# Cross-attention with RWKV: attention's projections emitted in halves between its other matrix pieces

## The chip, the cores and the metric

The kernel runs on one core of one Trainium2 chip. The metric is the device time of one launch in microseconds (us); lower is better. Three runs of the kernel before gave 1450.99, 1446.82 and 1450.00 us, so the median is 1450.0 us.

## What is computed

Sixteen sequences (B = 16) of 112 tokens of width 512 pass through two layers. The first is a gated cross-attention to 375 context rows per sequence with 16 heads of 32:

```python
a = layer_norm(audio_kv, gamma, beta)
Q = hidden @ Wq.T;  K = a @ Wk.T;  V = a @ Wv.T            # heads of 32
attn = softmax(where(mask, Q K^T * 32**-0.5, -inf))
x1 = hidden + tanh(gate) * ((attn V) @ Wo.T)
```

The second is an RWKV block on x1: a layer norm, a mix with the token before (a low-rank tanh network gives five mixtures), projections r, k, v, g and a decay w, then a recurrence over the tokens for each head, s = k v^T + w s, out = r (u k v^T + s), a group norm, an output projection, and a feed-forward part with its own layer norm and three 512x512 projections. Everything is float32.

## The kernel before

**Data and pools.** Activations lie transposed: 512 channels are four chunks (NC = 4) of 128 partitions, and the tokens are the free dimension. Two sequences make a group (GB = 2, N = 224 columns), eight groups in all. A float32 matmul of the program is two instructions in the profile; a transpose is one. PSUM has eight banks: two for the tag `mm` (`ps_mm`, every projection, every transpose of the context, the attention's output piece `po`, the transposed sums `pbc`, all norms), four for the tag `s` (`ps_s`, scores, transposed probabilities and the front's `pxm`), one for `acc` and one for `w`. A tile of `mm` holds its bank from its first matmul until the engine that reads it out has done so.

**Four streams.** `attention` is one generator over all 16 sequences. For each group follow `front` (layer norm and mixing), `middle` (the recurrence on VectorE and GpSimd, with its projections and the sums `acc` on TensorE) and `back` (group norm, output projection, feed-forward). Each generator yields a cost after a piece; the loop at the end of the kernel always resumes the stream whose place is least, and adds the cost times a rate to that place (ATT = 92.0, FRONT, MIDDLE, BACK). So the order in which the source emits pieces is a merge of the streams by these costs. The framework then fixes each engine's static order: earlier emitted work has priority, but an instruction whose inputs or buffer are not there yet in its plan lets later ones pass. Evacuations from PSUM are marked `high_priority`. On the chip each engine runs its fixed order, and a late input stops all that is behind it on that engine.

**A step of attention.** Step i works on sequence b = i // 4 and head block m = i % 4 (four heads, one chunk of channels). It emits:

1. `scores(b, m)`: four matmuls `ps` (L298) with 32 rows each, which run side by side in four row strips of the array; VectorE adds the mask and takes the minimum (L309).
2. `outputs` (L348) for the block two steps back: twelve matmuls `po` with 32 columns each, four side by side; ScalarE copies them out to `oR` (L353).
3. `exponentials` on ScalarE (L318), planned behind that copy.
4. `transposed` (L329) for the block one step back, three times (c = 0, 1, 2), four transposes `pt` each; ScalarE or VectorE copies them out as `prT` (L336, L338).
5. Units of dense work for the next sequence, a quarter of them in each step: four `turn` (L219, transposes `pa` of the context), four `key` (L234, `pk`, eight instructions of 375 columns), three `value` (L245, `pv`, eight of 512), and every other sequence two `query` units (`pq`, L180, sixteen of 224).

When a block with m = 3 has had its outputs, `divide` forms the reciprocal of the softmax sums (GpSimd, VectorE, and a GpSimd copy `spread`, L364), transposes that (`pbc`, L367) and multiplies it into the outputs (L375). After the second sequence of a group two `out_project` units (`pp`, L180) follow, and VectorE adds them to x (L278), which opens the group's `front`.

**Where the units stand before the change.** A step takes its share of units as a list `mine` (three or four, padded with empty ones). After `outputs` comes, in a step with a finished sequence, `mine[0]` and then the whole of `divide`. Then, whole: the first of the remaining units ahead of the transposes c = 0, the transposes c = 1 directly behind those of c = 0, the next unit ahead of c = 2, and what is left behind c = 2. Nothing is emitted between `scores` and `outputs`.

```python
for c in range(NSC):
    if c != 1:
        mine[c // 2][1]()
        yield mine[c // 2][0]
    prTs.append(transposed(bb, bm, c, bprs))
    yield 0.5
```

Of the kernel before, what the change touches and what calls it, by code (L numbers as in the profile page):

```python
# [1 line left out]

# [11 lines left out]
P = 128  # L14
# [4 lines left out]
GB = 2  # L19
# [30 lines left out]
def xattn_rwkv_kernel(ctx: ExitStack, tc: tile.TileContext, ins: dict, out: bass.AP):  # L50
# [99 lines left out]
    def slab(name, mm):  # L150
        w = slabs.tile([P, NC, 2 * P], F32, tag="slab", name=f"{name}_{mm}")
        load = (nc.sync if heads else nc.scalar).dma_start(w, ins[name][mm])
        if len(heads) >= 5:
            planned_after(load, heads[-3])
        return w
# [15 lines left out]
    def mm_tile(name):  # L171
        return ps_mm.tile([P, 512], F32, tag="mm", name=name)

    def project(name, mm, rhs, label):

        w = first.pop(0) if first else slab(name, mm)
        ps = mm_tile(label)
        for e in range(2):
            for k in range(NC):
                mm_ = nc.tensor.matmul(  # L180
                    ps[:, e * N : (e + 1) * N], w[:, k, e * P : (e + 1) * P], rhs[:, k, :],
                    start=(k == 0), stop=(k == NC - 1),
                )
                if e == k == 0:
                    heads.append(mm_)
        return ps[:, : 2 * N].rearrange("p (e n) -> p e n", e=2)


    projected = set()

# [20 lines left out]
    def context_units(b):  # L211

        raw = raws.pop(b)
        aT = ctxp.tile([P, NC, S], F32, tag="aT", name=f"aT_{b}")

        def turn(k):
            pt = mm_tile(f"pa_{b}_{k}")
            for c in range(NSC):
                nc.tensor.transpose(  # L219
                    pt[:, c * SC : (c + 1) * SC], raw[:, c, k * P : (k + 1) * P],  # L220
                    ident[:SC, :SC],
                )
            with tc.high_priority(AHEAD):
                nc.scalar.activation(
                    aT[:, k, :], pt[:, :S], AF.Identity, bias=vec(R_B0, k), scale=vec(R_G0, k)
                )

        kTs[b] = kT = []
        vs[b] = v = kvp.tile([SC, NSC, D], F32, tag="v", name=f"v_{b}")

        def key(m):
            pk = mm_tile(f"pk_{b}_{m}")
            for k in range(NC):
                nc.tensor.matmul(  # L234
                    pk[:, :S], wk[:, k, m * P : (m + 1) * P], aT[:, k, :],
                    start=(k == 0), stop=(k == NC - 1),
                )
            kT.append(kvp.tile([P, S], F32, tag="kT", name=f"kT_{b}_{m}", bufs=6))
            with tc.high_priority(AHEAD):
                nc.scalar.copy(kT[m], pk[:, :S])  # L240

        def value(c):
            pv = mm_tile(f"pv_{b}_{c}")
            for k in range(NC):
                nc.tensor.matmul(  # L245
                    pv[:SC, :], aT[:, k, c * SC : (c + 1) * SC], wv[:, k, :],
                    start=(k == 0), stop=(k == NC - 1),
                )
            with tc.high_priority(AHEAD):
                nc.scalar.copy(v[:, c, :], pv[:SC, :])  # L250

        return (
            [(0.5, lambda k=k: turn(k)) for k in range(NC)]
            + [(2.6, lambda m=m: key(m)) for m in range(NC)]
            + [(3.5, lambda c=c: value(c)) for c in range(NSC)]
        )

    def query_units(g):
        qTs[g] = qT = kvp.tile([P, NC, N], F32, tag="qT", name=f"qT_{g}")

        def query(mm):
            pq = project("wq", mm, xg[g], f"pq_{g}_{mm}")

            with tc.high_priority(AHEAD):
                nc.scalar.activation(  # L265
                    qT[:, 2 * mm : 2 * mm + 2, :], pq, AF.Copy, scale=-(HD ** -0.5)
                )

        return [(3.0, lambda mm=mm: query(mm)) for mm in range(2)]

    def project_units(g):
        oT = qTs[g]

        def out_project(mm):
            pp = project("wo", mm, oT, f"pp_{g}_{mm}")
            x = xg[g][:, 2 * mm : 2 * mm + 2, :]
            with tc.high_priority(AHEAD):
                nc.vector.scalar_tensor_tensor(x, pp, tgate, x, ALU.mult, ALU.add)  # L278
            if mm == 1:
                projected.add(g)  # L280

        return [(3.0, lambda mm=mm: out_project(mm)) for mm in range(2)]

    masks, dens, mns = {}, {}, {}

# [66 lines left out]
        with tc.high_priority(AHEAD):  # L352
            return nc.scalar.copy(oR[:, m, :], po[:, :T])  # L353

    def divide(b, oR):

        rden = sm.tile([T, H0], F32, tag="rden", name=f"rden_{b}")

        nan = sm.tile([T, H0], F32, tag="nan", name=f"nan_{b}", bufs=1)
        nc.gpsimd.tensor_scalar(nan, mns.pop(b), 1e9, 0.0, ALU.mult, ALU.mult)  # L360
        nc.vector.tensor_tensor(rden, dens.pop(b), nan, ALU.add)
        nc.vector.reciprocal(rden, rden)
        spread = sm.tile([T, H0, HD], F32, tag="spread", name=f"spread_{b}", bufs=1)
        nc.gpsimd.tensor_copy(spread, rden.unsqueeze(2).broadcast_to([T, H0, HD]))  # L364
        pb = mm_tile(f"pbc_{b}")
        for m in range(NC):
            nc.tensor.transpose(  # L367
                pb[:, m * T : (m + 1) * T],
                spread[:, 4 * m : 4 * m + 4, :].rearrange("p h d -> p (h d)"),
                ident[:T, :T],  # L370
            )
        t0 = (b % GB) * T

        with tc.high_priority(AHEAD):
            nc.vector.tensor_tensor(  # L375
                qTs[b // GB][:, :, t0 : t0 + T], pb[:, : NC * T].rearrange("p (m t) -> p m t", m=NC), oR,
                ALU.mult,
            )

    def attention():  # L380

        normalise(0)
        for cost, unit in query_units(0) + context_units(0):
            unit()
            yield cost
        load_ahead(1)
        normalise(1, heads[-1])
        units, before, ready, oR = [], None, None, None
        for i in range(NC * B + 2):
            b, m = divmod(i, NC)  # L390
            if i < NC * B:
                if m == 0:
                    g = b // GB
                    if b % GB == 0 and g + 1 < NG:
                        xg[g + 1] = load_x(g + 1)
                    if b + 1 < B:
                        units += context_units(b + 1)
                        if (b + 1) % GB == 0:
                            units += query_units(g + 1)
                prs, score = scores(b, m)  # L400
                if m == 2 and b + 2 < B:
                    load_ahead(b + 2, score)
                if m == 3 and b + 2 < B:
                    normalise(b + 2, score)
                yield 0.9
            copied = None
            if ready:
                bb, bm, prTs = ready
                if bm == 0:
                    oR = kvp.tile([P, NC, T], F32, tag="oR", name=f"oR_{bb}", bufs=1)  # L410
                copied = outputs(bb, bm, prTs, oR)
            if i < NC * B:
                exponentials(b, m, prs, copied)
            if ready:
                yield 0.8
            todo = -(-len(units) // (NC - m)) if i < NC * B else len(units)
            mine, units = units[:todo], units[todo:]
            mine = mine + [(0.0, lambda: None)] * (3 - len(mine))
            if ready and bm == NC - 1:
                mine[0][1]()  # L420
                yield mine[0][0]
                mine[0] = (0.0, lambda: None)
                divide(bb, oR)
                yield 0.6
                if bb % GB == GB - 1:
                    mine = mine[1:2] + project_units(bb // GB) + mine[2:]
            ready = None
            if before:
                bb, bm, bprs = before
                prTs = []  # L430
                for c in range(NSC):
                    if c != 1:
                        mine[c // 2][1]()
                        yield mine[c // 2][0]
                    prTs.append(transposed(bb, bm, c, bprs))
                    yield 0.5
                ready = bb, bm, prTs
                mine = mine[2:]
            for cost, unit in mine:
                unit()  # L440
                yield cost
            before = (b, m, prs) if i < NC * B else None
        for cost, unit in units:
            unit()
            yield cost
# [574 lines left out]
```

## Time and profile before

| | us |
|---|---|
| runs shown: median (lowest to highest) | 1450.0 (1446.82 to 1450.99) |
| the profiled execution, its own time | 1452.38 |
| its span, first to last instruction | 1450.5 |
| TensorE matmuls busy, of the span | 1342.6 (93%) |
| VectorE busy | 915.7 (63%) |
| ScalarE busy | 657.9 (45%) |
| GpSimd busy | 659.5 (45%) |
| mean granted TensorE clock | 0.968 |

How to read it: PE is TensorE's matmuls, PEld its weight loads, DVE VectorE, ACT ScalarE, POOL GpSimd. The profile covers one execution. A busy PE is a modelled figure: matmuls are pipelined, and the record of one is longer than its distance to the next, so stretches of work are measured here from start to start. The first 50 us load weights and prepare the first sequence; from about 270 to 1108 us the pattern repeats about every 168 us, once per group; attention's last matmul starts at 1237.53 us, and what follows belongs to the last groups' middle and back.

### The profile page before, as it was taken

How to read it: one execution, taken by the hardware profiler on the slowest of the kernel's cores; microseconds unless marked ns; L12 is line 12 of the kernel's file. 1: busy time of each engine (PE TensorE's matmuls, PEld its weight loads, DVE VectorE, ACT ScalarE, POOL GpSimd, SP SyncE). 2: the span in 40 equal slices, each digit the busy share in tenths (PEclk: the TensorE clock that was granted, in tenths of full speed). 3: DMA queues.
4: the chain of work that ended last, by engine and by line, in shares of the span. 5: the costliest groups of instructions: out<-in, count | busy, mean ns of one | idle time of the engine just before them, and what ended most of it. 6: DMA issues, size and time to landing. Idle time of an engine off the chain costs nothing.

```text
span 1450.5 us, 23365 instructions
## 1 busy us (share of the span) xinstructions
PE 1342.6 (93%) x8516; PEld 951.4 (66%) x8516; DVE 915.7 (63%) x1750; ACT 657.9 (45%) x1527; POOL 659.5 (45%) x639
## 2 busy tenths in 40 slices
PE   6999999999999999999999999999999898788777
PEld 4557575657676676757677576866767476567546
DVE  1344647884668747765757847686567638884852
ACT  1454442564436543455525644356535345423342
POOL 2000326742656336542555426563465516664750
PEclk8999999999999999999999999999999999989979
DMA  7212024513554045431554135451545124535541
GB/s 210 78 52 68 14 90 146 161 41 102 155 162 161 30 132 165 150 103 51 175 165 149 42 102 173 143 161 30 152 155 162 46 84 133 164 112 158 168 134 56
DMA packets 116587, 171.79 MB, mean 118 GB/s; under 512 B 9770, under 2 KB 89514, under 8 KB 116346
## 3 DMA queue, kind: packets, MB, share of 16 engines
q1 hardware_dynamic: 113578, 168.11, 37.9%
q10 hardware_dynamic: 2832, 2.10, 0.5%
q8 instruction: 67, 1.10, 0.3%
q14 instruction: 46, 0.38, 0.1%
q0 software_dynamic: 64, 0.10, 0.0%
HBM read 162.95 MB, written 7.34 MB: 117 GB/s over the span
## 4 chain that ended last, share of the span: by engine, by line
PE 68%; DVE 11%; DMA 7%; ACT 5%; POOL 4%; issue 3%; SPq 2%; DVEq 0%; ACTq 0%; POOLq 0%
PE pv L245 9%; PE pk L234 9%; PE pt L329 5%; PE ps L298 5%; DMA kv<-vd 4%; PE pfv L180 3%; PE pfk L180 3%; PE pfr L180 3%; PE po L180 3%; PE acc L770 3%; DVE st L754 3%; PE pq L180 3%; PE pr L180 2%; PE pg L180 2%; PE pv L180 2%
## 5 line engine op out<-in xcount | busy, mean ns | idle before, releaser
L758 POOL TENSOR_TENSOR st<-st,r 128x448 f32<-128x448 f32 x256 | 322.0, 1272 | 208.1 <-DVE st L754 200.7
L754 DVE TENSOR_TENSOR_SCAN st<-wp,kv 128x448 f32<-128x448 f32 x256 | 267.9, 1076 | 106.5 <-ACT qT L265 33.3
L731 POOL TENSOR_TENSOR kv<-kv,k 128x444 f32<-128x444 f32 x128 | 153.4, 1201 | 95.2 <-DMA kv<-vd 94.5
L234 PE MATMUL pk<-aT,wk 128*128 128x375 f32 x512 | 182.7, 501 | 12.0 <-ACT oR L353 11.1
L245 PE MATMUL pv<-wv,aT 128*125 128x512 f32 x384 | 175.6, 601 | 1.5 <-ACT v L250 1.0
L309 DVE CUSTOM_DVE_ANT_0 pr<-ps,mb 112x375 f32<-112x375 f32 x256 | 128.0, 542 | 58.2 <-PE ps L298 58.0
L318 ACT ACTIVATE pr<-pr,mn 112x375 f32<-112x375 f32 x256 | 153.1, 601 | 4.2 <-DVE mn L309 4.1
L234 PEld LDWEIGHTS pk<-aT,wk 128*128 128x128 f32 x512 | 97.4, 198 | 70.6 <-ACT oR L353 12.8
L329 PEld LDWEIGHTS pt<-ident,pr 112*125 112x125 f32 x768 | 103.2, 190 | 36.6 <-issue 16.2
L329 PE MATMUL pt<-ident,pr 112*125 112x112 f32 x768 | 114.2, 279 | 6.1 <-DVE xm L558 5.7
L245 PEld LDWEIGHTS pv<-wv,aT 128*125 128x125 f32 x384 | 68.8, 188 | 77.8 <-issue 73.7
L731 DVE TENSOR_TENSOR kv<-kv,k 128x444 f32<-128x444 f32 x128 | 108.8, 850 | 3.3 <-DMA kv<-vd 2.1
L770 PE MATMUL acc<-st,consts 128*32 128x224 f32 x1024 | 78.3, 374 | 11.0 <-POOL st L758 9.3
L298 PE MATMUL ps<-kT,qT 32*112 32x375 f32 x512 | 84.8, 528 | 1.8 <-DVE xm L558 0.9
L466 ACT ACT_TABLE_LOAD x64 | 82.1, 1283 | 1.1
L564 POOL TENSOR_TENSOR xm<-xm,xa 128x448 f32<-128x448 f32 x48 | 59.1, 1247 | 37.9 <-DVE xm L558 37.8
L338 DVE COPY prT<-pt 125x448 f32<-125x448 f32 x80 | 49.1, 614 | 42.5 <-PE pt L329 42.5
L336 ACT COPY prT<-pt 125x448 f32<-125x448 f32 x112 | 59.1, 528 | 28.0 <-PE pt L329 27.7
L290 POOL TENSOR_SCALAR mb<-mrow 112x375 f32<-112x375 uint8 x16 | 8.9, 556 | 132.6 <-DVE mn L309 132.0
L180 PE MATMUL pfk<-xk,wfk 128*128 128x224 f32 x256 | 55.9, 372 | 10.9 <-DVE xk L857 5.6
L558 DVE SCALAR_TENSOR_TENSOR xm<-pxm,vecs,sx 128x224 f32<-128x224 f32 x128 | 47.4, 442 | 29.1 <-PE pxm L581 29.1
L240 ACT COPY kT<-pk 128x375 f32<-128x375 f32 x64 | 30.0, 469 | 72.6 <-PE pk L234 71.8
(146 smaller groups left out, 2354.0 us busy)
## 6 DMA issues: line engine op xcount, KB each, us to landing
kv<-vd SPq DMA_DIRECT2D x512, 111.5 KB
wo<-in_wo SPq DMA_DIRECT2D x32, 512.0 KB
ctx<-in_ctx SPq DMA_DIRECT2D x15, 750.0 KB
wv<-in_wv SPq DMA_DIRECT2D x16, 512.0 KB
wk<-in_wk SPq DMA_DIRECT2D x16, 512.0 KB
wr<-in_wr SPq DMA_DIRECT2D x16, 512.0 KB
wg<-in_wg SPq DMA_DIRECT2D x16, 512.0 KB
wfk<-in_wfk SPq DMA_DIRECT2D x16, 512.0 KB
```

The lines of the kernel that those rows point to most:

```text
L180: mm_ = nc.tensor.matmul(ps[:, e * N : (e + 1) * N], w[:, k, e * P : (e + 1) * P], rhs[:, k, :], start=(k == 0), stop=(k == NC - 1),)
L234: nc.tensor.matmul(pk[:, :S], wk[:, k, m * P : (m + 1) * P], aT[:, k, :], start=(k == 0), stop=(k == NC - 1),)
L245: nc.tensor.matmul(pv[:SC, :], aT[:, k, c * SC : (c + 1) * SC], wv[:, k, :], start=(k == 0), stop=(k == NC - 1),)
L298: score = nc.tensor.matmul(ps[:T, :S], qT[r : r + HD, m, t0 : t0 + T], kT[r : r + HD, :], start=True, stop=True,)
L309: nc.vector.tensor_tensor_reduce(pr, pss[hh][:T, :S], mb, 1.0, 3.0e38, ALU.add, ALU.min, mn)
L318: exp = nc.scalar.activation(pr, pr, AF.Exp, bias=mns[b][:, h : h + 1], scale=-1.0, accum_out=dens[b][:, h : h + 1],)
L329: nc.tensor.transpose(pt[:SC, hh * T : (hh + 1) * T], prs[hh][:, c * SC : (c + 1) * SC], ident[:T, :T])
L466: nc.scalar.preload_act_table_set(table)
L731: product = engine.tensor_tensor(kv4[:, two(p), :, 1:T], kv4[:, two(p), :, 1:T], k_prev.unsqueeze(1).broadcast_to([P, 2, GB, T - 1]), ALU. ...
L754: scan = nc.vector.tensor_tensor_scan(flat(pair), w_ps[c], flat(kv[:, two(p), :]), 0.0, ALU.mult, ALU.add)
L758: nc.gpsimd.tensor_tensor(pair, pair, rs[c // 2][:, c % 2, :].unsqueeze(1).broadcast_to([P, 2, N]), ALU.mult,)
L770: part = nc.tensor.matmul(accs[c][32 * q : 32 * q + 32, :], consts[:, C_WIN + 32 * e : C_WIN + 32 * e + 32], st[:, q, :], start=(e == 0), ...
```

## The change

Key, value, query and output projections become two units each instead of one. A half of a key or value holds two of the four matmuls over the contraction, so its `mm` tile stays open between the halves; a half of a query or output projection holds one of its two blocks of 128 output columns, again in one tile. The copy out stays behind the second half. The halves' costs are half the old ones (1.3, 1.75, 1.5), so a sequence's sum is as before. The context's transposes (`turn`) stay whole.

A step now spreads its share of units evenly: some behind `scores`, some behind `outputs`, some behind each of the three groups of transposes, and some behind `divide`, mostly one half each. `divide` is cut in two: `sums_spread` (the GpSimd and VectorE part) is emitted directly behind `outputs`, and the rest behind the first group of transposes. The output projection's four halves are put behind the first unit that is then left.

```diff
+    def project_halves(cost, name, mm, rhs, label, then):
+        def half(e, state):
+            if e == 0:
+                state["w"] = first.pop(0) if first else slab(name, mm)
+                state["ps"] = mm_tile(label)
+            w, ps = state["w"], state["ps"]
+            for k in range(NC):
+                mm_ = nc.tensor.matmul(
+                    ps[:, e * N : (e + 1) * N], w[:, k, e * P : (e + 1) * P], rhs[:, k, :],
...
+            if e == 1:
+                then(ps[:, : 2 * N].rearrange("p (e n) -> p e n", e=2))
...
-        def key(m):
-            pk = mm_tile(f"pk_{b}_{m}")
-            for k in range(NC):
+        def key(m, half, state):
+            if half == 0:
+                state["ps"] = mm_tile(f"pk_{b}_{m}")
+            pk = state["ps"]
+            for k in (2 * half, 2 * half + 1):
...
+            todo = -(-len(units) // (NC - m)) if i < NC * B else len(units)
+            dense = deque(units[:todo])
+            units = units[todo:]
+            slots = 1 + (2 if ready else 0) + (NSC if before else 0)
+            slots += bool(ready and ready[1] == NC - 1)
+            def fill():
+                nonlocal slots
+                share = -(-len(dense) // slots)
+                slots -= 1
+                for _ in range(share):
+                    cost, unit = dense.popleft()
+                    unit()
+                    yield cost
+            yield from fill()
             copied = None
             if ready:
                 bb, bm, prTs = ready
...
             if ready:
+                if bm == NC - 1:
+                    sums_spread(bb)
                 yield 0.8
+                yield from fill()
+            last = ready and bm == NC - 1
+            ready = None
+            for c in range(NSC if before else 0):
+                if c == 0:
+                    prTs = []
+                if c == 1 and last:
+                    divide(bb, oR)
+                    yield 0.6
+                    if bb % GB == GB - 1:
+                        rest = list(dense)
+                        dense = deque(rest[:1] + project_units(bb // GB) + rest[1:])
+                    yield from fill()
+                prTs.append(transposed(*before[:2], c, before[2]))
+                yield 0.5
+                yield from fill()
```

More of the change, by code (lines that the diff above doesn't have):

```diff
@@ L1 @@
+from collections import deque
 from contextlib import ExitStack
@@ L186, in project @@
         return ps[:, : 2 * N].rearrange("p (e n) -> p e n", e=2)
+    def project_halves(cost, name, mm, rhs, label, then):
[7 more added lines that the diff above has]
+                    ps[:, e * N : (e + 1) * N], w[:, k, e * P : (e + 1) * P], rhs[:, k, :],
+                    start=(k == 0), stop=(k == NC - 1),
+                )
+                if e == k == 0:
+                    heads.append(mm_)
+            if e == 1:
+                then(ps[:, : 2 * N].rearrange("p (e n) -> p e n", e=2))
+        state = {}
+        return [(cost, lambda e=e: half(e, state)) for e in range(2)]
     projected = set()
@@ L237, in key, with value @@
                 )
[L238 to L244, printed above, removed]
+            if half == 1:
+                kT.append(kvp.tile([P, S], F32, tag="kT", name=f"kT_{b}_{m}", bufs=6))
+                with tc.high_priority(AHEAD):
+                    nc.scalar.copy(kT[m], pk[:, :S])
+        def value(c, half, state):
+            if half == 0:
+                state["ps"] = mm_tile(f"pv_{b}_{c}")
+            pv = state["ps"]
+            for k in (2 * half, 2 * half + 1):
                 nc.tensor.matmul(
@@ L248, in value, with halves @@
                 )
-            with tc.high_priority(AHEAD):
-                nc.scalar.copy(v[:, c, :], pv[:SC, :])
+            if half == 1:
+                with tc.high_priority(AHEAD):
+                    nc.scalar.copy(v[:, c, :], pv[:SC, :])
+        def halves(cost, part, i):
+            state = {}
+            return [(cost, lambda h=h: part(i, h, state)) for h in range(2)]
         return (
             [(0.5, lambda k=k: turn(k)) for k in range(NC)]
-            + [(2.6, lambda m=m: key(m)) for m in range(NC)]
-            + [(3.5, lambda c=c: value(c)) for c in range(NSC)]
+            + [half for m in range(NC) for half in halves(1.3, key, m)]
+            + [half for c in range(NSC) for half in halves(1.75, value, c)]
         )
@@ L259, in query_units, with copied @@
         qTs[g] = qT = kvp.tile([P, NC, N], F32, tag="qT", name=f"qT_{g}")
-        def query(mm):
-            pq = project("wq", mm, xg[g], f"pq_{g}_{mm}")
+        def copied(mm, pq):
             with tc.high_priority(AHEAD):
@@ L267, in query, with added @@
                 )
-        return [(3.0, lambda mm=mm: query(mm)) for mm in range(2)]
+        return [
+            half for mm in range(2)
+            for half in project_halves(
+                1.5, "wq", mm, xg[g], f"pq_{g}_{mm}", lambda pq, mm=mm: copied(mm, pq)
+            )
+        ]
     def project_units(g):
         oT = qTs[g]
-        def out_project(mm):
-            pp = project("wo", mm, oT, f"pp_{g}_{mm}")
+        def added(mm, pp):
             x = xg[g][:, 2 * mm : 2 * mm + 2, :]
@@ L280, in out_project @@
                 projected.add(g)
-        return [(3.0, lambda mm=mm: out_project(mm)) for mm in range(2)]
+        return [
+            half for mm in range(2)
+            for half in project_halves(
+                1.5, "wo", mm, oT, f"pp_{g}_{mm}", lambda pp, mm=mm: added(mm, pp)
+            )
+        ]
     masks, dens, mns = {}, {}, {}
@@ L353, in outputs, with sums_spread @@
             return nc.scalar.copy(oR[:, m, :], po[:, :T])
-    def divide(b, oR):
+    spreads = {}
+    def sums_spread(b):
         rden = sm.tile([T, H0], F32, tag="rden", name=f"rden_{b}")
@@ L362, in divide @@
         nc.vector.reciprocal(rden, rden)
-        spread = sm.tile([T, H0, HD], F32, tag="spread", name=f"spread_{b}", bufs=1)
+        spreads[b] = spread = sm.tile([T, H0, HD], F32, tag="spread", name=f"spread_{b}", bufs=1)
         nc.gpsimd.tensor_copy(spread, rden.unsqueeze(2).broadcast_to([T, H0, HD]))
+    def divide(b, oR):
+        spread = spreads.pop(b)
         pb = mm_tile(f"pbc_{b}")
@@ L414, in attention @@
             if ready:
+                if bm == NC - 1:
+                    sums_spread(bb)
                 yield 0.8
[L416 to L422, printed above, removed]
+                yield from fill()
[14 more added lines that the diff above has]
+                yield from fill()
+            if before:
+                ready = (*before[:2], prTs)
+            elif last:
                 divide(bb, oR)
@@ L425, in attention @@
                 if bb % GB == GB - 1:
[L426 to L439, printed above, removed]
+                    dense.extend(project_units(bb // GB))
+            while dense:
+                cost, unit = dense.popleft()
                 unit()
```

## The prediction

> **What bounds the kernel now.** I read the page's shares first, then the stages in the table of windows, then TensorE's waits, then single stretches of the timeline.
>
> ```profile
> PE 1342.6 (93%) x8516; PEld 951.4 (66%) x8516; DVE 915.7 (63%) x1750; ACT 657.9 (45%) x1527; POOL 659.5 (45%) x639
> PE   6999999999999999999999999999999898788777
> ```
>
> TensorE is busy in nine tenths or more of every slice from about 36 to 1120 us, and no other engine comes near it. The tail is different: 7s and 8s, a chain of the last groups' norms and recurrence.
>
> ```profile
> 436.00:604.00 168.00, 162.89 (x1078) 116.21 (x1077) 114.81 (x221) 84.69 (x199) 83.02 (x78) 1.00 0.40 125
> 1240.00:1450.00 210.00, 164.33 (x907) 129.97 (x906) 132.34 (x186) 73.24 (x134) 112.86 (x94) 0.90 0.43 132
> ```
>
> The columns are the window and its length, busy time of PE, PEld, DVE, ACT and POOL, granted clock, DMA share. One group's period of 168 us has 162.9 us of TensorE: about 5 us idle, 3%. Filling an idle array can win only those 5 us a period, and attention has no part in the last 210 us, which it only starts earlier or later. Which idle time is it?
>
> ```profile
> PE pk L234 <- ACT oR L353: 11.1, 5, 2.5
> PE ln_mean L488 <- POOL xa L483: 8.1, 7, 2.3
> PE pt L329 <- DVE xm L558: 5.7, 13, 0.9
> PE pfk L180 <- ACT v L250: 2.4, 4, 0.8
> PE pv L245 <- ACT v L250: 1.0, 1, 1.0
> PE pk L234 <- ACT kT L240: 0.8, 1, 0.8
> ```
>
> Each line gives who waited for whom, us in total, times, the longest. The first is no missing data: a key projection does not read oR. It waits for an `mm` bank, which the copy of `po` has to free. So do the last three; these four make 15.3 us. The second is the front's norm waiting for GpSimd, the third four `s` banks held by the front. Not one line shows a transpose waiting for exponentials or an output piece waiting for copies of the probabilities for longer than 0.9 us: **the pieces that the change puts work behind are already covered**, by whole units and by the other three streams.
>
> The long wait in the timeline, first TensorE, then ScalarE:
>
> ```profile
> 701.79 0.90 PE L298 MATMUL ps<-kT,qT 32*112 32x375 f32 x8
> 702.62 0.78 PE L348 MATMUL po<-prT,v 125*32 125x112 f32 x24
> 703.34 3.29 PE L180 MATMUL pk<-xm,wk 128*128 128x224 f32 x16
> 708.78 3.67 PE L234 MATMUL pk<-aT,wk 128*128 128x375 f32 x7 [2.15 <-ACT oR L353]
> ```
> ```profile
> 706.64 1.04 ACT L853 ACTIVATE xk<-xc,vecs,mix_by 128x222 f32<-128x222 f32 x2 [3.77 <-DVE xc L506]
> 707.58 1.02 ACT L853 ACTIVATE xr<-xc,vecs,mix_by 128x222 f32<-128x222 f32 x2
> 708.51 0.23 ACT L353 COPY oR<-po 128x112 f32<-128x112 f32 x1
> ```
>
> `po` was done near 703.4, but its copy stood on ScalarE behind `xk` and `xr`, which waited 3.77 us for VectorE. A whole projection of the middle (3.3 us) ran in the other bank meanwhile, and then TensorE had none. It recurs at 372, 540, 709, 879 and 1044 us.
>
> **The change part by part.** It adds and removes no instruction: 8516 matmul records, the same copies, the same weight loads. The yielded costs have the same sums, so the streams' shares stay. What changes is order.
>
> 1. *Work between `ps` and `po`.* In the timeline of the whole run I count `po` directly behind `ps` 41 times (of 64 output pieces). A change between full-array matmuls and pieces that use strips costs time because the next weights are not loaded under the running matmul:
>
> ```profile
> 607.87 3.21 PE L180 MATMUL pp<-qT,wo 128*128 128x224 f32 x16
> 611.00 0.59 PE L770 MATMUL acc<-st,consts 128*32 128x224 f32 x8
> ```
> ```profile
> 191.49 3.03 PE pv L180 x16
> 194.51 3.03 PE pk L180 x16
> ```
>
> Sixteen instructions of 224 columns take 3.13 us to a strip piece's start (611.00 - 607.87) and 3.02 to another dense one's (194.51 - 191.49, chain of work): 0.11 us for the change, call it 0.10. `ps` to `po` pays one (rows to columns); `ps`, half, `po` pays two. So 41 x 0.10 = **+4.1 us**, all on TensorE's path; at most 64 x 0.10 = 6.4 if every step is split, and 0 if the planned order leaves no half there. The Trainium skill, in "TensorEngine Tiling (Array Packing)", section Key Properties, says that changing the tiling mode drains TensorE, which speaks against this edit and agrees in kind; it gives no price there. The page "TensorE: Matmul & The Clock Gate", Part 2, puts a drain at about 128 cycles, an estimate of 0.05 us, and the term would be about 2 us by it; the measured 0.10 goes into my sum.
>
> 2. *Halves behind transposes.* Four `pt` take 0.43 us before a dense piece (690.46 to 690.89) and eight take 0.86 between dense pieces (743.70 to 744.56 in the timeline): 0.11 each either way. No price: 0.
>
> 3. *An `mm` bank stays open between two halves.* This is the new wait. Before, a unit took a bank, filled it in 2.7 to 3.5 us, and the other bank was copied out meanwhile. Now a half holds one of two banks while `po`, `pbc` or another stream's projection goes through the other. There are 18 split units per group (8 keys, 6 values, 2 queries, 2 outputs), some 135 windows in the run once the first sequence is set up. `po` falls between two halves when a unit's first half stands behind `scores`, in about half of 62 steps: 30. Other streams take 30 `mm` tiles per group (front 4, middle 14, back 12, from the source) among attention's about 88 yields, 0.34 a yield, 0.7 in a window of two yields; so in about half of the 30, 15 times, a third tile asks for a bank while both are held. What waits behind it on TensorE is everything: it is one queue. If the static order runs the second half first, the price is 0. If not, it is at least the copy that frees the bank: 0.25 us for oR, 0.47 for kT, 0.53 to 0.59 for the others (the tiles' rows), and at most what the trace shows when ScalarE is late, 11.1/5 = 2.2 us. Ends: 0 and 15 x 2.2 = 33 us. I take kT's 0.47, because an order planned around buffers leaves the plain copy more often than a blocked ScalarE: 15 x 0.47 = **+7 us**.
>
> 4. *The existing bank waits.* The finer order may move the five coincidences apart, or make them worse: with a half as cover (1.3 us) instead of a whole projection (3.3), a copy that is 5 us late costs up to 2 us more each, 5 x 2.0 = +10. If they go, -11.1 us, and also clock: the granted clock in the 4 us behind the pauses at 372, 709 and 1044 was 0.57, 0.61 and 0.57, behind the other two 1.00. Three times some 1.7 us, -5 us. I take 0, since what causes them is VectorE's and ScalarE's order, which isn't touched. The Trainium skill ("TensorE: Matmul & The Clock Gate", Part 1) says that the clock falls after an idle window of about 3.4 us; here pauses of 2.15 to 2.45 us were followed by it. By the page pauses of this length cost no clock and the gain would be 11 us, by the trace 16.
>
> 5. *`sums_spread` earlier.* The same GpSimd copy (0.61 us) and VectorE pair (0.15 and 0.25 at 1222) move ahead of about two halves and one transposed group. They are queued ahead of some recurrence work, in which GpSimd is idle half the time (82 to 83 us busy of 168), so nothing is late. TensorE's `pbc` waits 0.3 us in all. Gain at most 0.3, loss at most 16 x 1.0 = 16 us if each delayed the recurrence and TensorE had no cover; I take 0.
>
> 6. *Weight loads.* wq and wo loads are issued on SP's queue at the first half, 30 loads moved by a few pieces among 512 recurrence loads. TensorE waits for a weight once, at the start (4.0 us). Covered; a 512 KB load at the 120 GB/s of the windows lasts 4.3 us, the price of one that came late. 0, with one or two of these in the range.
>
> Copies after key, value and query, and VectorE's additions after the output projection, stay behind the second half; what waits for them stays.
>
> Sum: 4.1 + 7 = +11 us, in the stretch to 1237 us, and the tail starts that much later. The profiled execution's own time is 1452.4 (span 1450.5), 2.4 above the median, so 1463 for such an execution and **1461** beside the median of 1450.
>
> **Rivals.** (a) *Better cover, faster.* Small dense pieces between all strips mean that the next bank request is never far behind a copy; the five pauses and their half-speed clock go, -16, against +4 for the changes of mode: -12, **1438**. For it: the pauses are coincidences of order, and order is what changes. Against: the other idle lines (the norm behind GpSimd, the front's four banks) do not touch attention's units, and the ceiling is 5 us a period. (b) *One bank instead of two.* Part 3 at its upper end, when ScalarE is late as at 708 us: 33 + 4 = +37, **1487**. It decides from more than about 5 of 15 cases being late. (c) *The order hardly changes*: the framework's plan already lets ready work pass, so halves come together again and the strips stay side by side: **1450**. Against: priorities follow emission, and the timeline shows pieces largely in emitted order.
>
> **How the numbers follow.** A measurement of this kernel can tell about 0.3% (4.35 us) from no change. Forecast of about +11, with all slower outcomes below the rival's: 0.42; (b) 0.12; (a) 0.35; (c) 0.11. Faster 0.35, same 0.11, slower 0.54. The signs are nearly balanced, because the pauses are coincidences. Within slower the likeliest range is 1455 to 1475. The range for 8 in 10 must take in (a) with one period's other 5 us gained, 1433, and (b), 1487.
>
> **What would show it.** Right: `ps` followed by a half and then `po` in most steps, and more changes between dense and strip pieces; more or longer TensorE waits on the copies oR, kT, v, qT or on other streams' evacuations; about the same `ln_mean` and `pxm` waits; periods of 169 to 170 us instead of 168. Wrong: the line "pk <- oR" gone with nothing in its place and periods below 167 (rival a), or `ps` and `po` still side by side (c). A change of the tail alone (after attention's last matmul) by more than 5 us would come from a cause that I haven't priced.

## The result, and the profile after

Four runs of the changed kernel have a median of 1521.7 us (1520.1 to 1526.6), four of the kernel before beside them 1448.4 us. The ratio is 1.051, with a 95% interval of 1.048 to 1.054: **slower by 5%**, 73 us. The sign of the forecast was right; the time lies well above its range (1433 to 1487). The profiled execution took 1522.3 us, with a span of 1520.5, so the two profiles are 70.0 us apart.

The first view is the page of the changed kernel: busy time by engine, TensorE's busy share in 40 slices, and the clock granted to it.

```profile
PE 1381.6 (91%) x8516; PEld 968.9 (64%) x8516; DVE 926.2 (61%) x1750; ACT 662.2 (44%) x1528; POOL 673.9 (44%) x639
PE   7999998999999899988999899998999889789787
PEclk8899999999999899998999999999999999989788
```

The number of matmuls is the same, but 39 us more of busy time stand in it, and more slices show an 8. Neither tells where the time went, so the next views are tables of windows: one group's period in the kernel before, then the same period and the last 210 us in the changed kernel (the columns are those of the prediction's table).

```profile
457.12:624.61 167.49, 161.30 (x1060) 115.14 (x1060) 113.19 (x216) 82.97 (x193) 83.01 (x79) 1.00 0.41 126
```
```profile
482.76:663.05 180.29, 168.03 (x1060) 118.54 (x1060) 114.07 (x217) 83.85 (x193) 84.73 (x79) 0.96 0.38 116
1310.00:1520.00 210.00, 169.46 (x893) 131.85 (x892) 136.75 (x187) 74.87 (x137) 114.38 (x94) 0.86 0.42 130
```

A period is the stretch from one group's front norm (`ln_mean`) to the next one's; its start is called a mark here. The same 1060 matmuls take 180.3 us, where the kernel before needs 167.5, and the granted clock is 0.96 instead of 1.00. The tail looks as before. Measured by these marks, the span's 70 us split into +25.6 up to the third mark, +46.4 in the four periods that follow (671.3 to 717.7) and -2 behind them. The loss is a toll on every group that overlaps attention.

I split the four periods by TensorE's records from start to start. Of the +46.4 us, **+30.0 are pauses** of over 0.15 us (19 pauses with 19.3 us before, 41 with 49.3 after), and **+16.0 are clock**: TensorE ran at half clock, outside pauses, for 13.6 us before and 45.6 after, and half of such a time is lost. All that is left, counted at full clock, stayed (645.2 us before, 645.7 after). So TensorE has no more work; it stands more often, and runs slowly behind that.

Who is waited for? The list of TensorE's waits in the changed kernel gives who waited for whom, us in total, times, the longest.

```profile
PE ln_mean L553 <- POOL xa L548: 11.7, 7, 1.9
PE pxm L646 <- DVE mn L349: 10.2, 5, 2.0
PE gm L690 <- DVE rden L403: 9.5, 5, 2.2
PE pfr L181 <- DVE own L762: 9.1, 5, 1.8
PE pt L369 <- DVE xm L623: 7.8, 8, 2.0
PE po L388 <- ACT k L721: 6.5, 5, 1.3
PE ps L338 <- ACT prT L376: 4.6, 6, 0.9
```

The old first line, `pk` behind `oR`, is gone. The wait for GpSimd's `xa` is still there (8.1 us before; in the four periods 6.3 before and 6.9 after). The other lines are new or have grown, and most come five times, once a group. By what ends them, the pauses per period are, in us before and after: an `mm` bank 2.6 and 3.9, an `s` bank 0.7 and 4.4, data 1.7 and 3.9. Only the first kind was priced.

**Two of the new pauses in the timeline** of the changed kernel. TensorE first; the brackets hold the pause ahead of an instruction and what ended it.

```profile
681.79 0.69 PE L369 MATMUL pt<-ident,pr 112*125 112x112 f32 x4
684.72 1.69 PE L690 MATMUL gm<-o,consts 128*128 128x448 f32 x2 [2.24 <-DVE rden L403]
...
699.38 0.88 PE L338 MATMUL ps<-kT,qT 32*112 32x375 f32 x2 [0.64 <-DVE mn L349]
699.85 1.11 PE L646 MATMUL pxm<-th,maa 32*128 32x224 f32 x8
702.99 1.86 PE L646 MATMUL pxm<-th,maa 32*128 32x224 f32 x8 [2.03 <-DVE mn L349]
```

And VectorE in the same stretch:

```profile
682.09 1.46 DVE L226 TENSOR_SCALAR ctx<-ctx,mv,rs 125x512 f32<-125x512 f32 x3 [1.09 <-POOL rs L224]
683.46 0.81 DVE L599 SCALAR_TENSOR_TENSOR mx<-sx,vecs,xa 128x224 f32<-128x224 f32 x2
684.19 0.38 DVE L843 TENSOR_TENSOR o<-acc,own 128x224 f32<-128x224 f32 x1
...
701.85 0.62 DVE L699 TENSOR_TENSOR o<-o,gsq 128x448 f32<-128x448 f32 x1 [1.59 <-ACT gsq L536]
702.39 0.54 DVE L349 CUSTOM_DVE_ANT_0 pr<-ps,mb 112x375 f32<-112x375 f32 x1
```

The group norm's matmul `gm` reads `o`. (The wait is put down to `rden`, which merely comes next on VectorE; `gm` starts 0.15 us after `o` is done.) `o` is an addition of 0.38 us whose sums `acc` TensorE had finished at 681.8. But on VectorE it stands behind the context's normalisation (`ctx`, L226), which waits for a GpSimd reciprocal root, and behind `mx`. In the kernel before the order is another. First TensorE, then VectorE:

```profile
640.44 0.96 PE L770 MATMUL acc<-st,consts 128*32 128x224 f32 x16
...
642.14 1.02 PE L625 MATMUL gm<-o,consts 128*128 128x448 f32 x2
```
```profile
641.47 0.39 DVE L778 TENSOR_TENSOR o<-acc,own 128x224 f32<-128x224 f32 x1 [0.98 <-PE acc L770]
...
648.89 1.46 DVE L204 TENSOR_SCALAR ctx<-ctx,mv,rs 125x512 f32<-125x512 f32 x3 [1.31 <-POOL rs L202]
```

`acc` is done at 641.4, `o` follows at once, `gm` starts without a pause, and the normalisation comes only at 648.9.

The second pause is one of `s` banks. `pxm` needs a bank which the last score minimum of four (L349) must free. Three minima are done by 700.3; the fourth stands behind `o<-o,gsq`, which waits 1.59 us for ScalarE. TensorE stands for 2.03 us, for an instruction of 0.54.

Now the clock behind these pauses, by the table of windows of the changed kernel (the number behind the five busy times is the granted clock):

```profile
685.00:689.00 4.00, 4.00 (x14) 2.69 (x17) 0.62 (x1) 1.88 (x3) 0.61 (x1) 0.59 0.02 4
703.00:707.00 4.00, 4.00 (x36) 2.73 (x37) 3.50 (x9) 2.49 (x4) 3.10 (x3) 0.50 0.00 0
```

TensorE is busy in every moment of both windows, at about half speed. In the four periods that is nearly all of its additional busy time (16.0 of 17.5 us).

Last, the pause that halving itself makes, in the timeline of the changed kernel:

```profile
779.71 1.78 PE L198 MATMUL pq<-x,wq 128*128 128x224 f32 x8
...
782.36 1.02 PE L760 MATMUL pruk<-own,consts 128*128 128x448 f32 x2
783.21 1.68 PE L198 MATMUL pq<-x,wq 128*128 128x224 f32 x8
786.71 3.29 PE L181 MATMUL pfr<-xr,wfr 128*128 128x224 f32 x16 [1.82 <-DVE own L762]
```

The first half of `pq` holds one `mm` bank from 779.7, and `pruk` takes the other. ScalarE has copied `pq` out by 785.5, yet `pfr` starts only when VectorE has read `pruk` out (`own`, done at 786.65). So `pfr` seems to be planned for that bank, and stands even while the other is free.

### The profile page after: what moved, and what is told of

The parts are those of the page before. It is cut to its first block, busy times and chain, and to the rows that moved or that the text cites. A ratio compares the mean times of both kernels' runs of the same rounds, so it can differ in the third digit from the quotient of the medians.

```text
span 1520.5 us, 23383 instructions
## 1 busy us (share of the span) xinstructions
PE 1381.6 (91%) x8516; PEld 968.9 (64%) x8516; DVE 926.2 (61%) x1750; ACT 662.2 (44%) x1528; POOL 673.9 (44%) x639
## 4 chain that ended last, share of the span: by engine, by line
PE 58%; DVE 17%; DMA 8%; ACT 5%; issue 5%; POOL 4%; SPq 2%; DVEq 0%; ACTq 0%; POOLq 0%
PE pk L258 10%; PE pv L272 7%; DMA kv<-vd 5%; DVE st L819 4%; PE pt L369 4%; PE pfr L181 3%; PE po L181 3%; PE pr L181 3%; PE pfv L181 2%; PE ps L338 2%; PE po L388 2%; PE acc L835 2%; PE pv L181 2%; PE pa L241 2%; PE pfk L181 2%
## 5 line engine op out<-in xcount | busy, mean ns | idle before, releaser
L258 PE MATMUL pk<-aT,wk 128*128 128x375 f32 x512 | 198.7, 510 | 0.1
L272 PE MATMUL pv<-wv,aT 128*125 128x512 f32 x384 | 188.0, 611 | 1.2 <-ACT oR L393 1.2
L796 POOL TENSOR_TENSOR kv<-kv,k 128x444 f32<-128x444 f32 x128 | 157.7, 1233 | 27.6 <-ACT prT L376 26.0
L349 DVE CUSTOM_DVE_ANT_0 pr<-ps,mb 112x375 f32<-112x375 f32 x256 | 127.0, 542 | 61.4 <-PE ps L338 61.4
L369 PEld LDWEIGHTS pt<-ident,pr 112*125 112x125 f32 x768 | 108.6, 191 | 47.2 <-issue 24.9
L258 PEld LDWEIGHTS pk<-aT,wk 128*128 128x128 f32 x512 | 92.5, 197 | 58.0 <-issue 22.3
L369 PE MATMUL pt<-ident,pr 112*125 112x112 f32 x768 | 118.3, 277 | 7.8 <-DVE xm L623 7.8
L835 PE MATMUL acc<-st,consts 128*32 128x224 f32 x1024 | 83.9, 379 | 8.2 <-DVE o L843 4.5
L338 PE MATMUL ps<-kT,qT 32*112 32x375 f32 x512 | 77.5, 524 | 10.7 <-ACT prT L376 4.6
L198 PE MATMUL pq<-x,wq 128*128 128x224 f32 x256 | 61.0, 385 | 8.8 <-DVE own L762 4.6
L181 PE MATMUL pfr<-xr,wfr 128*128 128x224 f32 x256 | 56.0, 375 | 13.3 <-DVE own L762 9.1
```

Source lines behind the costliest of these rows:

```text
L181: mm_ = nc.tensor.matmul(ps[:, e * N : (e + 1) * N], w[:, k, e * P : (e + 1) * P], rhs[:, k, :], start=(k == 0), stop=(k == NC - 1),)
L258: nc.tensor.matmul(pk[:, :S], wk[:, k, m * P : (m + 1) * P], aT[:, k, :], start=(k == 0), stop=(k == NC - 1),)
L272: nc.tensor.matmul(pv[:SC, :], aT[:, k, c * SC : (c + 1) * SC], wv[:, k, :], start=(k == 0), stop=(k == NC - 1),)
L338: score = nc.tensor.matmul(ps[:T, :S], qT[r : r + HD, m, t0 : t0 + T], kT[r : r + HD, :], start=True, stop=True,)
L349: nc.vector.tensor_tensor_reduce(pr, pss[hh][:T, :S], mb, 1.0, 3.0e38, ALU.add, ALU.min, mn)
L369: nc.tensor.transpose(pt[:SC, hh * T : (hh + 1) * T], prs[hh][:, c * SC : (c + 1) * SC], ident[:T, :T])
```

## The experiments

The change does four things at once, and each gives a theory. **Halving**: open `mm` banks between halves cost the time. **Places**: work now stands behind `scores`, behind `outputs` and between every two groups of transposes, so the `s` banks of a step are asked for at other times. **Division**: the sums are spread early and divided late. **Shares**: counted in halves, a first step takes five of 18 units, the four context transposes and a half, where it took three of eleven; so the steps' amounts of work differ. A fifth theory is that the rates of the merge (ATT against the other streams) merely fit the old source. Against all these stands a sixth: every edit of the order moves VectorE's and ScalarE's fixed orders, and no one part holds the loss.

Beside each ratio to the kernel before (95% interval) stand the pauses per period by kind (`mm` bank / `s` bank / data, in us; before 2.6 / 0.7 / 1.7, after 3.9 / 4.4 / 3.9) and the length of the period (167.8 and 179.4).

**1. Halves in the old places.** Both halves of a unit back to back where the whole stood, with a yield behind each (`run` emits the pieces of one unit so); the old division, the old shares.

```diff
-                        mine[c // 2][1]()
-                        yield mine[c // 2][0]
+                        yield from run(mine[c // 2])
```

> The changed kernel's halves, but both halves of a unit stand one behind the other at the places that whole units had before, with a yield between them; sums and division stand as before. Theory H (an open bank between halves makes the pauses): 1490 us or more, since another stream can still step between the halves. Theory P (the new places make them): 1445 to 1462. Theory S (any change of the merged order costs, whatever it is): 1480 or more.

Measured: 1464.9 us, 1.010 (1.007 to 1.013); pauses 5.7 / 0.3 / 2.1, period 170.4. The list of TensorE's waits of this kernel:

```profile
PE pk L258 <- ACT oR L393: 13.5, 5, 2.9
PE pfr L181 <- DVE own L743: 12.0, 5, 2.4
```

The old wait is still there, and `pfr` behind `own`, which the kernel before lacks, is added. So halving in the old places costs 1%, through `mm` banks (2.6 to 5.7).

**2. Whole units in the new places.** The changed kernel, with the two halves of a unit handed out as one.

```diff
-        return [(cost, lambda e=e: half(e, state)) for e in range(2)]
+        return [(2 * cost, lambda: [half(e, state) for e in range(2)])]
```

> Whole units again, but handed out by the changed kernel's rule: behind scores, behind outputs, behind single groups of transposes; sums early, division late. Theory H: no tile is open between pieces, so 1465 us or less. Theory P: 1490 or more. Theory S: 1480 or more.

Measured: 1521.8 us, 1.049 (1.046 to 1.052); pauses 5.4 / 0.4 / 5.4, period 180.8. As slow as the change, with no unit halved. Halving alone as the cause fell with these two. Pauses and clock make only 7.6 of the 13.0 us by which this period is longer than before. Some 4 more lie in the score matmuls, which more often start one behind the other than side by side (0.18 us from one to the next on average, 0.10 before), without a pause that counts.

**3 and 4. The rate of attention**, 96 instead of 92, in the kernel before and in the changed one; later also 88 in the changed one.

```diff
-ATT = 92.0
+ATT = 96.0
```

> The kernel before with one constant changed: attention's merge rate 1/96 instead of 1/92, so that all pieces stay whole and at their places in attention, and only the merge with the other streams shifts. Theory S: 1480 us or more, as far as the changed kernel. Theories H and P: within 1.5% of 1450, 1428 to 1472.

> The changed kernel with the same constant, 1/96. Theory S: its order is matched to no rate yet, so another rate may give back 20 us or more, 1500 or less. Theories H and P: the pauses come from attention's own sequence, so 1505 to 1540 at any rate near this.

> The changed kernel at the other side, attention's rate 1/88. With 1/92 it takes 1522, with 1/96 1514. Theory S in the form that the changed order only lacks a matched rate: 1490 or less at one of them. If the changed order is itself the worse one: 1500 to 1545 at every rate.

Measured: 1481.8 us, 1.021 (1.016 to 1.026) for the kernel before with 96; 1513.6, 1.045 (1.040 to 1.050) and 1539.6, 1.063 (1.057 to 1.068) for the changed one with 96 and 88. An edit that touches no piece of attention costs 2%, with pauses of 3.3 / 1.0 / 4.0. Of the three rates tried none brings the changed kernel near 1450. So a lost fit of 92 is not the whole of it, while other rates stay untried.

**5 and 6. One part taken out of the change**: no share behind `scores`; or the old division in one piece, behind `outputs` and one share.

```diff
-            slots = 1 + (2 if ready else 0) + (NSC if before else 0)
+            slots = (2 if ready else 0) + (NSC if before else 0)
...
-            yield from fill()
             copied = None
```
```diff
                 yield 0.8
                 yield from fill()
             last = ready and bm == NC - 1
+            if last:
+                sums_spread(bb)
+                divide(bb, oR)
...
-                if c == 1 and last:
-                    divide(bb, oR)
```

> The changed kernel without its share of dense work between scores and outputs; the other shares grow. Theory P1 (the work behind scores is what hurts: the output piece and its copy, the exponentials and the transposes all come later): 1485 us or less. Theory P2 (the early sums and the late division hurt): 1505 or more. Theory P3 (dense work between single groups of transposes hurts): 1505 or more.

> The changed kernel with sums and division together, behind outputs and one share, as before. Theory P2: 1485 us or less. Theories P1 and P3: 1505 or more.

Measured: 1517.7 us, 1.045 (1.042 to 1.048), pauses 6.2 / 1.1 / 3.5; and 1503.1 us, 1.035 (1.032 to 1.038), pauses 5.4 / 4.3 / 1.1. Neither gives back a third. In the first most waits for `s` banks go and `mm` waits come in their place; in the second most of the late data go and `mm` waits grow.

**7, 8 and 9. One part put into the kernel before**, with whole units: the first unit of a step between `scores` and `outputs`; sums early and division late; a unit between c = 0 and c = 1 instead of ahead of c = 2.

```diff
+            if before:
+                mine[0][1]()
+                yield mine[0][0]
+                mine[0] = (0.0, lambda: None)
             copied = None
```
```diff
             if ready:
+                if bm == NC - 1:
+                    sums_spread(bb)
                 yield 0.8
...
                     prTs.append(transposed(bb, bm, c, bprs))
                     yield 0.5
+                    if c == 0 and last:
+                        divide(*last)
```
```diff
-                    if c != 1:
-                        mine[c // 2][1]()
-                        yield mine[c // 2][0]
+                    if c != 2:
+                        mine[c][1]()
+                        yield mine[c][0]
```

> The kernel before with one edit: the first whole unit of a step stands between scores and outputs instead of behind outputs. Theory P1: 1490 us or more. Theories P2 and P3: 1465 or less. Theory S (half of the loss is any disturbance of an order that was matched to the rates): about 1480, as for the other merge rate.

> The kernel before with one edit: the sums directly behind outputs, the division behind the first group of transposes. Theory P2: 1485 us or more. Theories P1 and P3: 1465 or less. Theory S: about 1480.

> The kernel before with one edit: the second whole unit stands ahead of the second group of transposes instead of the third, so that the last two groups come one behind the other, nearer to the next scores. Theory B (the four s banks: the last group's banks are not copied out when scores or the front ask for four, so what counts is the dense work behind the transposes): 1475 us or more, with TensorE waits for the copies of transposes, scores or mixtures. Theory S (any change of a matched order costs about 30): about 1480 with no such lines. If neither: 1445 to 1460.

Measured: 1492.0 us, 1.027 (1.024 to 1.030), pauses 5.2 / 0.2 / 4.0; 1453.1 us, 1.001 (0.999 to 1.003), pauses 3.3 / 0.7 / 0.7; 1446.1 us, 0.997 (0.995 to 0.999), pauses 2.6 / 0.3 / 3.2. Work between the scores and the outputs costs 2.7% by itself; by the fifth run, taking it out of the change gives back only 0.6 points. The early sums cost nothing, and a unit between the first transposes costs nothing either, which had been my explanation of the `s` waits.

**10, 11 and 12. The places of the changed kernel taken back**, all with the old division: without the share behind `scores`; with nothing between c = 0 and c = 1; with both.

```diff
-            slots = 1 + (2 if ready else 0) + (NSC if before else 0)
+            slots = 1 + (2 if ready else 0) + (NSC - 1 if before else 0)
...
                 prTs.append(transposed(*before[:2], c, before[2]))
                 yield 0.5
-                yield from fill()
+                if c:
+                    yield from fill()
```

> The changed kernel with the division as before and without the share behind scores: what is left is halves, one behind outputs and one behind each group of transposes. Theory B: the even spreading alone holds most of the loss, 1490 us or more. Theory A (the parts add: the share behind scores is worth about 4, the division about 19): 1495 to 1502. If the share behind scores is the main part in the absence of the others, as in the kernel before with one unit moved: 1470 or less.

> The changed kernel with the division as before and no dense work between the first two groups of transposes; the share behind scores stays. Theory B: 1485 us or less. Otherwise, if the share behind scores is enough by itself as in the kernel before with one unit moved: 1490 to 1505.

> The changed kernel with all three new places taken back: division as before, nothing behind scores, nothing between the first two groups of transposes; halves and the rule that hands them out stay. Should stand with the halves in the old places, 1455 to 1475 us; if it stays above 1490, the halves or the rule hold a loss that the first experiment did not show.

Measured: 1519.6 us, 1.046 (1.044 to 1.049); 1564.3 us, 1.079 (1.075 to 1.083); 1538.8 us, 1.061 (1.058 to 1.063). Pauses 4.6 / 4.2 / 4.6, 8.0 / 3.3 / 6.4 and 4.8 / 1.4 / 5.7. The last is nearer to the old places than the change is, and slower than it. Places as the only cause fell here. The twelfth shows an old acquaintance at the head of its list of TensorE's waits:

```profile
PE gm L684 <- DVE mv L221: 23.6, 5, 4.7
```

It is the same `o` as above. In this kernel's timeline VectorE adds it at 687.15, behind four score minima, the context's statistics and `sx`, which had waited 1.86 us for ScalarE; TensorE stands for 4.7 us.

**13, 14 and 15. Shares.** The changed kernel with units counted whole, so that the four steps of a sequence take 3, 3, 3 and 2 of them as before (4, 3, 3 and 3 with the queries); the twelfth kernel with this count; and the kernel before with one more unit in a sequence's first step.

```diff
-            todo = -(-len(units) // (NC - m)) if i < NC * B else len(units)
+            todo = len(units)
+            if i < NC * B:
+                turns = sum(1 for cost, _ in units if cost == 0.5)
+                whole = -(-(turns + (len(units) - turns) // 2) // (NC - m))
+                todo = whole + max(0, whole - turns)
```
```diff
-            todo = -(-len(units) // (NC - m)) if i < NC * B else len(units)
+            todo = -(-len(units) // (NC - m)) + (m == 0) if i < NC * B else len(units)
```

> The changed kernel, but each step takes as many units as before, counted whole (a turn is one, two halves are one: 3, 3, 3, 2 or 4, 3, 3, 3), so that no unit is begun in one step and ended in the next. Places and halves stay. Theory C (the count in pieces moves work between steps and leaves a bank open into the next step): 1475 us or less. Theory P (the places within a step): 1500 or more.

> The same old shares in the kernel with all three new places taken back, which took 1539 us with the new shares. Theory C: 1475 us or less, as with halves in the old places. If it stays above 1500, the rule that spreads a step's pieces holds the loss, or any order far from the matched one does (theory S).

> The kernel before with whole units at their old places and one more unit in the first step of each sequence (4, 3, 2, 2 or 5, 3, 3, 2). Theory C in its form that the shares alone matter: 1490 us or more. If only the open bank matters: 1465 or less. Theory S: about 1480.

Measured: 1494.5 us, 1.030 (1.025 to 1.034), pauses 2.9 / 2.5 / 4.5; 1533.9 us, 1.056 (1.050 to 1.062), pauses 6.4 / 2.7 / 2.5; 1502.4 us, 1.035 (1.029 to 1.039), pauses 2.5 / 3.5 / 1.7. The old shares give back 2.1 points of the 5, and one more unit in the first step alone costs the kernel before 3.5%, with the `s` waits that the change shows too. The list of TensorE's waits in the fifteenth kernel:

```profile
PE ps L298 <- ACT prT L336: 7.4, 10, 1.6
...
PE gm L625 <- DVE o L778: 5.8, 6, 1.1
PE pxm L581 <- ACT prT L336: 5.5, 5, 1.1
```

But the fourteenth, with the old places, the old division and the old shares, is as slow as ever. It differs from the first (1.010) in the rule that hands out a step's share. Halves are counted evenly, so that a unit may stay open across a group of transposes, or across the four halves of an output projection; by the same rule some units stand a place earlier or later. Between the two lie 4.6 points.

**16 and 18. Two small edits together**: the eighth and ninth in the kernel before; and the ninth's place in the first.

> The kernel before with the two edits that alone cost nothing (sums early and division behind the first transposes, 1.0008; second unit ahead of the second group of transposes, 0.9971). Whole units, old shares. If edits of order add: 1440 to 1452 us. Theory S (each order has pauses of its own, and edits do not add): anything from 1440 to 1490.

> Halves one behind the other, as in the first experiment (1465), with the second unit ahead of the second group of transposes, which alone gave 1446. If halves cost some 16 us in themselves: 1458 to 1468. Theory S: 1446 to 1500, not foreseeable from the two.

Measured: 1444.5 us, 0.995 (0.993 to 0.998), pauses 2.8 / 0.3 / 2.3; and 1460.4 us, 1.006 (1.004 to 1.009), pauses 6.1 / 0.3 / 2.6. The sixteenth, early sums and a whole unit between the first transposes, beats both kernels, by half a per cent against the one before. The eighteenth against the ninth gives the price of halving back to back again: 0.9 points, and `mm` waits of 6.1 where 2.6 stood.

**What holds in all of them.** The period less its pauses and less half of its time at half clock lies between 159 and 167 us in every kernel; it is about 161 before, in the change and in the tenth, and 159 in the slowest. So there pauses and clock carry the difference. They don't everywhere: it is 167 in the second and 166 in the seventeenth. And the wait of `gm` for the addition `o` on VectorE goes with the loss in most kernels, which doesn't show that it makes it: 1.0 to 1.2 us in a run in the kernel before and in the first, eighth, ninth, sixteenth and eighteenth, which lie within 1.0% of it or are faster; 4.4 to 26.8 us in twelve of the other fourteen kernels, all slower by 2% or more (13.0 in the change). The sixth and the seventeenth, at 1.3 and 1.0, lose their time at other waits.

Shown, then: the loss of the change is pauses and the clock behind them. Two of the pauses, 17.1 of the 49.3 us in the four periods, are followed to VectorE's order; that the others come of VectorE's and ScalarE's orders too is argued from what ended them, and no run held these orders fixed. Shown too: halving back to back costs 1%, and each of three other things (a unit behind the scores, the shares, the merge rate) costs 2 to 3.5% alone, while they do not add: taking one back leaves most of the loss, and taking three back can make it worse. **Open** is which edit moves which instruction: several suffice, and the framework's planning stands between the source and the order. The splitting of a unit across other pieces, which may hold the difference between the first and the fourteenth, was not tried by itself.

## Why the prediction was right in sign and wrong in size

**What bounds the kernel** held. TensorE sets the end, and its work at full speed didn't change. The sign was right, but largely by luck: the prediction itself had it nearly balanced, and the two terms of its sum come, on balance, to some 12 of the 70 us.

**Step 1, changes of mode: right.** `po` directly behind `ps` fell from 41 times to 0, and the changes between modes rose from 495 to 526 in the run; 31 times 0.10 is an estimate of +3.1 us, where +4.1 stood.

**Step 2 and step 6: right**; no such wait shows, and TensorE's wait for `wq` stays at the start.

**Step 3, the open bank: right in kind, too small.** New `mm` pauses of 3.9 us a period came (`pfr` behind `own` 1.8, `po` behind `k` 1.3, and smaller ones), some 27 us if seven periods are alike, where +7 stood between the ends 0 and 33. The old ones, 2.6 us a period, went, which step 4 had left in place. The balance, +1.3 us a period or some +9, lies near +7 by luck. Halving in the old places raised the `mm` pauses by 3.1 us a period (first run) and the time by 1%.

**Step 4 failed.** It said "I take 0, since what causes them is VectorE's and ScalarE's order, which isn't touched". That order is touched. Nothing in the diff names these engines, but their instructions are emitted with the pieces, and the planner sets one order from all of them. In the two stretches shown, a score minimum came to stand behind the group norm's work, and the normalisation of the next context moved ahead of `o`. Three terms were missing, per period: `s` banks +3.7 us, late data +2.2, and the clock behind all of it, +4.0; together 9.9 of the 11.6 us that a period grew. The bounds of this step, -16 and +10, were drawn from the five pauses that the trace had; new pauses cannot be bounded by the old ones. The step saw the clock, but only as a gain. The Trainium skill ("TensorE: Matmul & The Clock Gate", Part 1), which ties the fall to an idle window of about 3.4 us, differs from the trace here again: no pause of the four periods is longer than 2.25 us, and 16.0 us of the loss are clock.

**Step 5, sums earlier: right alone** (1.001 in the eighth run), though in the changed kernel the old division gives back 1.6 points.

**Not priced at all: the shares.** The prediction said that the costs "have the same sums, so the streams' shares stay". Over a sequence they do; within it, counting halves moves work to its first step, and one more unit there alone cost 3.5% in the kernel before.

**The rivals.** (a) needed the five pauses to go; they went, and others came in their place. (b) named a mechanism that is there, and its new pauses come near its price (27 of 33 us), but the old ones went at the same time. (c) is excluded: the order changed more than I thought. None of the three had a pause for any buffer but `mm`, or for data.

**What would show it.** The stated signs mostly came (`ps`, half, `po`; more waits on copies; `ln_mean` in the four periods about as before), but the `pxm` wait, which I expected to stay, grew to 10.2 us, and the periods are 179, not 169 to 170. The halving alone, in the first run, has 170.4.

## What to carry to other kernels

Where a planner or a merge sets all the engines' orders from the order of emission, no edit moves one engine alone: list what stands ahead of each short instruction that a bank or a matmul waits for, on every engine, and every pool of banks, not only the one that the diff names. A kernel that stands for 3% of its time has little to win by finer interleaving and much to lose by a new order, so a forecast of such an edit should put the price of *some* new pauses ahead of the gain (here 2 to 3.5% for three of the five single edits of the kernel before, and nothing for the other two). And test a split alone, in its old place, before it is spread: here it cost 1%, which no new place that was tried paid back.

## What the runs showed of the hardware

Short pauses cost clock too. In the four periods of the changed kernel, each stretch at half clock lasts 3.41 or 6.83 us. All four pauses of 2.24 to 2.25 us (`gm`) and two of the four of some 1.68 us (`ln_mean`) were followed by 3.41 us of it. Each cluster of three pauses of 0.88, 0.64 and 2.03 us within 8 us had 6.83, from within or close behind its last pause. Where the clock falls, a pause of 2 us so costs 3.7 us, and a cluster of 3.6 us costs 7. It isn't certain: behind all four pauses of 1.82 to 1.84 us (`pfr`), and behind two of the five pauses of some 2.2 us in the kernel before (at 540 and 879 us), the clock stayed at 1.00. So the length of a single pause doesn't decide it here. What does was not tried.
